# Selective-scan layer of a four-layer network: scan in double steps with its first states in a column of the tile, mean and residual moved to TensorE

## The chip, the cores and the metric

The kernel runs on one core of a Trainium2 chip. The time is device microseconds of one execution; the time of a version is the median of its runs. A profile is of one execution, whose own time is given beside its span. The engines are named PE (TensorE), DVE (VectorE), ACT (ScalarE), POOL (GpSimd) and SP (SyncE, which here only issues DMAs).

## The reference

A network of four residual layers on x of shape (3, 256, 48, 48), fp32: `x = x + layer(groupnorm(x))`. Layer 0 is a block with attention, layer 1 a convolution with mixed kernels, layer 2 a plain convolution. Layer 3, which the change touches, is a selective scan (Mamba) over the 2304 pixels of each image, taken as a sequence; cut to what matters:

```
xn    = layernorm over the 256 channels
x_in  = in_proj(xn)[:512];  z = in_proj(xn)[512:]
u     = silu(causal convolution of x_in, 4 taps)
dt_raw, B, C = x_proj(u)                 # 16, 16 and 16 rows
dt    = softplus(dt_proj(dt_raw) + bias)
# for each of 512 channels d and 16 states n, over time t:
h[d,n] = h[d,n] * exp(dt[d] * A[d,n]) + dt[d] * B[n] * u[d]
y[d]   = sum over n of h[d,n] * C[n]
out   = out_proj((y + u * D) * silu(z))
```

## The kernel before, in words

Layers 0 to 2 come first (lines 344 to 990) and are not touched. Layer 3 begins at line 995. Each image is cut into 6 chunks of 384 pixels (`CH`), 18 chunks in all, in the order of `todo`. The 512 channels are four blocks `m`; the 16 states are four groups `g` of four. A scan works on 128 partitions: 32 channels by 4 states of the group, so that block m and group g need four scans, `q` = 0 to 3. A **step** is (chunk, m, g): 16 steps a chunk, 288 steps.

For one step:

- `fill` (line 1285) makes the scan's second input dt * u * B in a tile `hs` of four rows of 384. DVE writes q 0 and 1 from PSUM (`ps_r`, which `spread_pe`, line 1268, makes with PE by replicating channels); POOL writes q 2 and 3 from SBUF (`dtur`, which `spread`, line 1258, brings by DMA from a copy in DRAM, together with `dtr` for the decays).
- `decay` (line 1296): ACT writes exp(dt * A) of one q into a PSUM tile; three such tiles take turns, so ACT is up to three scans ahead.
- Line 1360: DVE's scan of one q, in place in `hs`. Its start is 0.0 in the first chunk of an image, else a column of `hst`, which ACT copied from the same step's last column in the chunk before (line 1372).
- Line 1375: POOL multiplies the whole `hs` with C into `hc`.
- `add_states` (line 1309): PE sums over states, four matmuls of 32 output rows into `ps_y`, after a first one that adds u * D. It is called two steps later. `gate` (line 1325) multiplies with silu(z) on DVE.

In the program's order a step is: fill of the next step, spread_pe (at g = 2), four scans with the decay three scans ahead behind each, the copy to hst, the product with C, add_states of the step two before.

Between them lie the stages that prepare the next two chunks and finish the one before. Lists written out by hand (lines 1207 to 1251) give each stage the step number j of the chunk (0 to 15), a place in the step (MID: after the second scan; LATE: after the product with C; PE_: at the step's end) and the chunk it works for. Among them, for the chunk two ahead, layer norm: `group_scale` (ACT, j 12), `channel_mean` (PE, j 12), `centre` (DVE subtracts the mean from `xg`, ACT squares, j 13), `channel_mean` of the squares (PE, j 13), `inverse_root` (ACT), `normalise` (DVE), `tokens` (ACT). For the next chunk: `taps` (convolution and input projection as eight matmuls of PE for each block) and `take_u` (ACT), `silu` (ACT: a table load, the Silu, a table load back), `project_u`, `take_dbc` (ACT and DMAs of B and C), `project_dt`, `softplus` (three ACT passes), `take_dt` (DVE, then an ACT copy, then DMAs), `project_z`, `take_z`. For the chunk before: `residual` (DMA of x into `ot`), `project_y` (PE), `store` (DVE adds `ot`, DMA out). All these matmuls use one pair of PSUM banks, `bank` (`ps_g`).

`keep_order` (line 1397) fixes on PE, DVE, ACT and POOL exactly the order in which the program writes the instructions. So what counts on each engine is what stands ahead in its queue. The helper `run` (line 1253) calls the stages of a place in the order of the lists.

Of the kernel before, what the change touches and what calls it, by code (L numbers as in the profile page):

```python
# [9 lines left out]
F32 = mybir.dt.float32  # L10
I32 = mybir.dt.int32
AF = mybir.ActivationFunctionType
ALU = mybir.AluOpType
AX = mybir.AxisListType
PSUM = bass.MemoryType.PSUM

P = 128
# [3 lines left out]
CT = 2  # L21
# [4 lines left out]
CH = 384  # L26
NCH = N // CH
# [7 lines left out]
DI = 4  # L35
# [47 lines left out]
def net(  # L83
# [20 lines left out]
    nc = tc.nc  # L104
# [13 lines left out]
    def v(name, i=0, n=1):  # L118
# [3 lines left out]
    ident = const.tile([P, P], F32, name="ident")  # L122
# [6 lines left out]
        out=gview, in_=gview, pattern=[[-8, 16], [0, 8]], compare_op=ALU.is_ge,  # L129
# [3 lines left out]
        out=gview, in_=gview, pattern=[[8, 16], [0, 8]], compare_op=ALU.is_ge,  # L133
# [4 lines left out]
    mean2 = const.tile([P, P], F32, name="mean2")  # L138
# [205 lines left out]
    with ExitStack() as l0:  # L344
# [39 lines left out]
        with ExitStack() as p1:  # L384
# [3 lines left out]
            for b in ORDER:  # L388
# [12 lines left out]
                for m in range(2):  # L401
                    for ct in range(CT):
                        nc.tensor.matmul(
                            pb[:, m : m + 1], w("cv1", ct * 256 + m * P, P), sh[:, ct : ct + 1],
                            start=ct == 0, stop=ct == CT - 1,
                        )
                bb = small.tile([P, 2], F32, name="bb")
# [3 lines left out]
                for c in range(NCH):  # L411
                    for m, dst in ((0, y1), (1, cur[b])):
                        pm = ps.tile([P, 512], F32, tag="s", name="ps_y")
                        for ct in range(CT):
                            nc.tensor.matmul(
                                pm[:, :CH], ws[:, ct, m * P : (m + 1) * P], chunk(xb[:, ct, :], c),
                                start=ct == 0, stop=ct == CT - 1,
# [67 lines left out]
        with ExitStack() as p2:  # L485
# [9 lines left out]
            for i in range(NB):  # L495
# [268 lines left out]
                for mt in range(0, NT, 2):  # L764
                    pv = pair()
                    for j in range(2):
                        nc.tensor.matmul(
                            pv[:, j, :384], cur[2][:, (mt + j) * P : (mt + j + 1) * P], wn[2],
                            start=True, stop=True,
# [19 lines left out]
                if i + 1 < NB:  # L789
# [4 lines left out]
                    for b in ORDER:  # L794
                        for c in range(NCH):
                            f = hidden(b, c)
# [67 lines left out]
        i = NB - 1  # L864
        mark = listed[-1]
        chunks = [(b, c) for b in ORDER for c in range(NCH)]
# [15 lines left out]
        for n, b in enumerate(ORDER):  # L882
            held = None
            for c in range(NCH):
                f = hidden(b, c)
# [31 lines left out]
    with ExitStack() as l1:  # L917
# [55 lines left out]
        for n, (k, h) in enumerate(halves):  # L973
            layer, b = units[k]
# [17 lines left out]

    with ExitStack() as l3:
        wp = l3.enter_context(tc.tile_pool(name="w3", bufs=1))
        act = l3.enter_context(tc.tile_pool(name="act", bufs=2))
        scn = l3.enter_context(tc.tile_pool(name="scn", bufs=2))
        psd = l3.enter_context(tc.tile_pool(name="psd", bufs=3, space=PSUM))
        psr = l3.enter_context(tc.tile_pool(name="psr", bufs=1, space=PSUM))  # L1000
        psg = l3.enter_context(tc.tile_pool(name="psg", bufs=1, space=PSUM))
        psy = l3.enter_context(tc.tile_pool(name="psy", bufs=1, space=PSUM))
# [32 lines left out]
            )  # L1035
        fold = rep[:, 0, :]

        diag = wp.tile([P, DI, P], F32, name="diag")
        for m in range(DI):
            nc.vector.tensor_scalar(diag[:, m, :], ident, v("D", m), None, ALU.mult)  # L1040
# [3 lines left out]
        def fetch(at):  # L1044
            k = chunks[at] = Chunk()
            k.b, k.c = todo[at]
            k.before = chunks.get(at - 1)
            k.xg = act.tile([P, CT, CH], F32, name="xg")
            nc.sync.dma_start(k.xg, xd[k.b][:, :, k.c * CH : (k.c + 1) * CH])
# [14 lines left out]
                    bias=sh[:, ct : ct + 1], scale=sc[:, ct : ct + 1],  # L1064
                )

        def channel_mean(src, j):
            for ct in range(CT):
                nc.tensor.matmul(  # L1069
                    bank[:, j, :CH], mean2, src[:, ct, :], start=ct == 0, stop=ct == CT - 1  # L1070
                )

        def centre(k):
            mu = bank[:, 0, :CH].unsqueeze(1).broadcast_to([P, CT, CH])
            nc.vector.tensor_tensor(k.xg, k.xg, mu, ALU.subtract)
            k.sq = act.tile([P, CT, CH], F32, name="sq", bufs=1)
            nc.scalar.activation(k.sq, k.xg, AF.Square)

# [107 lines left out]
        def project_y(k, mo):  # L1186
            for m in range(DI):
                nc.tensor.matmul(  # L1188
                    bank[:, mo, :CH], w("out", m * 256 + mo * P, P), k.sz[:, m, :],
                    start=m == 0, stop=m == DI - 1,  # L1190
                )

        def residual(k):
            k.ot = act.tile([P, CT, CH], F32, name="ot")
            nc.sync.dma_start(k.ot, xd[k.b][:, :, k.c * CH : (k.c + 1) * CH])

        def store(k, mo):
            o = k.ot[:, mo, :]
            nc.vector.tensor_tensor(o, bank[:, mo, :CH], o, ALU.add)  # L1199
            nc.sync.dma_start(  # L1200
                out[k.b, mo * P : (mo + 1) * P, k.c * CH : (k.c + 1) * CH], o
            )

        MID, LATE, PE_ = range(3)
        plan = [
            (12, MID, 2, group_scale),
            (12, PE_, 2, lambda k: channel_mean(k.xg, 0)),
            (13, MID, 2, centre),  # L1210
            (13, PE_, 2, lambda k: channel_mean(k.sq, 1)),
            (14, MID, 2, inverse_root),
            (14, LATE, 2, normalise),
            (15, MID, 2, tokens),
# [22 lines left out]
            (4, MID, -1, residual),  # L1237
            (6, PE_, -1, lambda k: project_y(k, 0)),
            (6, PE_, -1, lambda k: project_y(k, 1)),
            (7, LATE, -1, lambda k: store(k, 0)),  # L1240
            (7, LATE, -1, lambda k: store(k, 1)),
        ]

        gating = [
# [8 lines left out]
        def run(at, j, place):  # L1253
            for when, where, rel, stage in after + plan + gating:
                if (when, where) == (j, place) and 0 <= at + rel < len(todo):
                    stage(chunks[at + rel])

        def spread(k, m):

            dtr = scn.tile([P, 4, CH], F32, name="dtr")  # L1260
            dtur = scn.tile([P, 2, CH], F32, name="dtur")
            for i in range(4):
                r = slice(32 * i, 32 * i + 32)
                nc.sync.dma_start(dtr[r], k.dtd[:, m, :].rearrange("(q d) n -> d q n", d=32))
                nc.sync.dma_start(dtur[r], k.dtud[:, m, :].rearrange("(q d) n -> d q n", d=32))
            return dtr, dtur
# [10 lines left out]
            k.ps = t  # L1277


        steps = [(at, m, g) for at in range(len(todo)) for m in range(DI) for g in range(4)]  # L1280
        chunks = {}
        tiles = {}
        state = {}

        def fill(s):

            at, m, g = steps[s]
            k = chunks[at]
            bb = k.bc[0][:, g, :].unsqueeze(1).broadcast_to([P, 2, CH])
            hs = tiles[s] = scn.tile([P, 4, CH], F32, name="hs", bufs=4)  # L1290
            nc.vector.tensor_tensor(hs[:, 0:2, :], k.ps[:, :, :CH], bb, ALU.mult)  # L1291
            nc.gpsimd.tensor_tensor(hs[:, 2:4, :], k.rows[m][1], bb, ALU.mult)  # L1292

        decays = []

        def decay(n):

            s, q = divmod(n, 4)
            if s >= len(steps):
                return  # L1300
            at, m, g = steps[s]
            da = psd.tile([P, 512], F32, tag="d", name="ps_da")
            col = (m * 4 + g) * 4 + q
            nc.scalar.activation(  # L1304
                da[:, :CH], chunks[at].rows[m][0][:, q, :], AF.Exp, scale=amat[:, col : col + 1]
            )
            decays.append(da)

        def add_states(s):

            at, m, g = steps[s]
            k = chunks[at]
            hc = tiles.pop(s)
            if g == 0:
                k.y_ps = psy.tile([P, 512], F32, name="ps_y")
                nc.tensor.matmul(
                    k.y_ps[:, :CH], diag[:, m, :], k.u[:, m, :], start=True, stop=False
                )
            for q in range(4):
                nc.tensor.matmul(  # L1320
                    k.y_ps[32 * q : 32 * q + 32, :CH], fold, hc[:, q, :],
                    start=False, stop=g == 3,
                )

        def gate(at, m):
            k = chunks[at]
            nc.vector.tensor_tensor(k.sz[:, m, :], k.y_ps[:, :CH], k.sz[:, m, :], ALU.mult)
# [17 lines left out]
        for _, _, _, stage in gating:  # L1345
            stage(k)

        for s, (at, m, g) in enumerate(steps):
            k = chunks[at]
            j = 4 * m + g  # L1350
            if j == 2 and at + 2 <= last:
                fetch(at + 2)
            if s + 1 < len(steps):
                fill(s + 1)

            if g == 2 and s + 2 < len(steps):
                spread_pe(chunks[steps[s + 2][0]], steps[s + 2][1])
            hs = tiles[s]
            for q in range(4):
                nc.vector.tensor_tensor_scan(  # L1360
                    hs[:, q, :], decays[q][:, :CH], hs[:, q, :],
                    0.0 if k.c == 0 else state[m, g][:, q : q + 1], ALU.mult, ALU.add,
                )
                decay(4 * s + q + 3)
                if q == 1:
                    if g == 2 and s >= 6:
                        gate(*steps[s - 6][:2])
                    run(at, j, MID)
            del decays[:4]
            if k.c < NCH - 1:  # L1370
                h = state[m, g] = wp.tile([P, 4], F32, name=f"hst{m}{g}")
                nc.scalar.copy(h.unsqueeze(2), hs[:, :, CH - 1 : CH])
            cb = k.bc[1][:, g, :].unsqueeze(1).broadcast_to([P, 4, CH])
            hc = tiles[s] = scn.tile([P, 4, CH], F32, name="hc", bufs=3)
            nc.gpsimd.tensor_tensor(hc, hs, cb, ALU.mult)  # L1375
            run(at, j, LATE)
            if s >= 2:
                add_states(s - 2)
            run(at, j, PE_)
            if g == 1 and m + 1 < DI:  # L1380
                k.rows[m + 1] = spread(k, m + 1)
            elif g == 1 and at < last:
                chunks[at + 1].rows = {0: spread(chunks[at + 1], 0)}
        end = len(steps) - 1
        add_states(end - 1)
        add_states(end)
        gate(*steps[end][:2])
        k = chunks[last]
        residual(k)
        for mo in range(2):  # L1390
            project_y(k, mo)
        for mo in range(2):
            store(k, mo)
        keep_order(tc, listed, mark)


# [110 lines left out]
```

## Time and profile before

| | |
|---|---|
| median of 3 runs | 3835.44 us (3830.97 to 3836.76) |
| the profiled execution | 3840.89 us, span 3839.1 us |
| busy in the span | PE 84%, DVE 84%, ACT 58%, POOL 40% |
| mean granted clock of PE | 0.901 |
| first fill of POOL in layer 3 | at 2245.35 us |
| first scan, end of the last scan | 2257.74 us, 3819.57 us |
| DMA | 266.50 MB, mean 69 GB/s |

The page gives the busy time of each engine, then forty slices of the span with the busy share in tenths, DMA queues, the chain that ended last, and the costliest groups of instructions. A group's line has the source line, the engine, the operation, out<-in with shapes, how often, then the busy time in us and the mean ns of one, and after the second bar the idle time of the engine just before these instructions and what ended it. A timeline line has start and length in us, the engine, the line and the operation, and how many were merged. Times in a timeline are from the start of the span.

### The profile page before, as it was taken

The numbers are of one execution on the slowest core, as the hardware profiler recorded it, in microseconds if no ns is written. First come the engines' busy times: TensorE is split into PE (matmuls) and PEld (weight loads), VectorE is DVE, ScalarE is ACT, GpSimd is POOL, SyncE is SP. The second block draws the span as 40 slices with busy tenths as digits, with TensorE's granted clock in tenths as the row PEclk, the third lists the DMA queues.
The fourth block names the chain that finished last, engine by engine and source line by source line (L and its number), as shares of the span: only waits on it lengthen the run. The fifth ranks groups of instructions, "written<-read, shape, count | busy, mean of one in ns | idle before, by whom it ended". The sixth has DMA issues, their size and how long they took to land. (4 is left out here: it accounts for less than half of the span.)

```text
span 3839.1 us, 45642 instructions
## 1 busy us (share of the span) xinstructions
PE 3232.1 (84%) x17010; PEld 1406.6 (37%) x17010; DVE 3221.5 (84%) x3518; ACT 2228.0 (58%) x3216; POOL 1554.8 (40%) x674
## 2 busy tenths in 40 slices
PE   7999999999999988677699757777878878777874
PEld 4323232432323234355577523333333333333331
DVE  4898989779899963799988349999999999999997
ACT  2788787668878762210000147666677666667763
POOL 0000000000000002100000039999999999999998
PEclk9999999999999999888899878888888888888886
DMA  4000000000000015555101133434443433343441
GB/s 170 3 1 1 1 2 1 26 13 1 1 1 2 1 57 173 174 177 177 45 25 42 59 71 100 105 99 104 103 104 91 108 91 99 100 112 92 111 100 34
DMA packets 149962, 266.50 MB, mean 69 GB/s; under 512 B 23441, under 2 KB 123601, under 8 KB 147170
## 3 DMA queue, kind: packets, MB, share of 16 engines
q1 hardware_dynamic: 137634, 245.80, 22.9%
q10 hardware_dynamic: 12096, 17.70, 1.4%
q8 instruction: 135, 2.21, 0.2%
q14 instruction: 97, 0.79, 0.1%
HBM read 216.31 MB, written 46.89 MB: 69 GB/s over the span
## 5 line engine op out<-in xcount | busy, mean ns | idle before, releaser
L587 ACT ACTIVATE pt<-ps_s 128x1024 f32<-128x1024 f32 x972 | 939.0, 1022 | 237.3 <-PE ps_s L583 219.9
L1375 POOL TENSOR_TENSOR hc<-hs,bc 128x1536 f32<-128x1536 f32 x288 | 991.4, 3443 | 85.6 <-DVE hs L1360 56.7
L663 DVE TENSOR_TENSOR part<-part,pt 128x2048 f32<-128x2048 f32 x396 | 906.6, 2289 | 78.4 <-ACT pt L587 53.8
L1360 DVE TENSOR_TENSOR_SCAN hs<-ps_da,hst,hs 128x384 f32<-128x384 f32 x960 | 909.8, 997 | 23.5 <-ACT ps_da L1304 19.9
L1304 ACT ACTIVATE ps_da<-dtr,amat 128x384 f32<-128x384 f32 x1152 | 657.1, 581 | 359.0 <-DVE hs L1360 339.9
L160 POOL TENSOR_TENSOR rstd<-ve,mhalf 128x2 f32<-128x2 f32 (+1 forms) x26 | 17.5, 675 | 1661.7 <-DVE ve L158 1661.7
L583 PE MATMUL ps_s<-q,kt 32*128 32x512 f32 (+1 forms) x4320 | 616.4, 595 | 2.3 <-DVE q L544 0.9
L1292 POOL TENSOR_TENSOR hs<-dtur,bc 128x768 f32<-128x768 f32 x288 | 523.8, 1819 | 77.5 <-DMA dtr<-dtd 77.5
L596 PE MATMUL acc<-pt,vt 128*32 128x512 f32 (+1 forms) x4320 | 523.5, 563 | 8.2 <-DVE o L643 8.0
L927 PE MATMUL ps_c<-vt,u 128*128 128x288 f32 x1728 | 437.8, 417 | 92.9 <-DVE u L257 55.1
L1105 PE MATMUL ps_g<-xn,wtap 128*128 128x384 f32 x1152 | 392.2, 493 | 36.3 <-ACT u L1112 31.3
L927 PEld LDWEIGHTS ps_c<-vt,u 128*128 128x128 f32 x1728 | 335.4, 195 | 190.0 <-issue 56.3
L583 PEld LDWEIGHTS ps_s<-q,kt 32*128 32x128 f32 x4320 | 220.2, 184 | 389.6 <-issue 230.0
L1320 PE MATMUL ps_y<-hc,rep 128*32 128x384 f32 x2304 | 293.5, 596 | 34.6 <-POOL hc L1375 32.7
L1291 DVE TENSOR_TENSOR hs<-ps_r,bc 128x768 f32<-128x768 f32 x288 | 269.1, 934 | 61.8 <-PE ps_r L1273 61.8
L1105 PEld LDWEIGHTS ps_g<-xn,wtap 128*128 128x128 f32 x1152 | 212.7, 189 | 220.1 <-ACT u L1112 54.9
L596 PEld LDWEIGHTS acc<-pt,vt 128*32 128x32 f32 x4320 | 95.7, 108 | 364.3 <-issue 328.5
L943 ACT COPY cb<-ps_c 128x288 f32<-128x288 f32 x48 | 19.0, 395 | 355.5 <-PE ps_c L927 258.5
L1360 DVE TENSOR_TENSOR_SCAN hs<-ps_da,hs 128x384 f32<-128x384 f32 x192 | 170.7, 937 | 17.9 <-ACT ps_da L1304 17.7
L1176 PE MATMUL ps_g<-xn,w3sb 128*128 128x384 f32 x288 | 133.8, 608 | 58.1 <-ACT sz L1184 43.3
L1069 PE MATMUL ps_g<-xg,mean 128*128 128x384 f32 x72 | 52.7, 887 | 105.3 <-ACT dt L1167 78.2
L1320 PEld LDWEIGHTS ps_y<-hc,rep 128*32 128x32 f32 x2304 | 51.3, 118 | 239.1 <-POOL hc L1375 113.5
(204 smaller groups left out, 3265.5 us busy)
## 6 DMA issues: line engine op xcount, KB each, us to landing
wconv<-in_we SPq DMA_DIRECT2D x144, 384.0 KB, 4.3
dtr<-dtd SPq DMA_DIRECT2D x288, 192.0 KB, 3.6
bc<-bcd SPq DMA_DIRECT2D x144, 192.0 KB, 5.9
dtur<-dtud SPq DMA_DIRECT2D x288, 96.0 KB, 2.7
dtd<-dt SPq DMA_DIRECT2D x18, 768.0 KB, 3.5
yc<-ycat ACTq DMA_DIRECT2D x18, 576.0 KB, 5.3
xb<-in_x SPq DMA_DIRECT2D x6, 1152.0 KB, 11.1
ycat<-cur SPq DMA_DIRECT2D x6, 1152.0 KB, 4.9
```

The lines of the kernel that those rows point to most:

```text
L583: nc.tensor.matmul(s[:, j, cols], kt[r, mt * P : (mt + 1) * P], q[r, :n], start=True, stop=True,)
L587: nc.scalar.activation(p[:, h0 : h0 + 2, :], s, AF.Exp)
L596: nc.tensor.matmul(acc[h * HD : (h + 1) * HD, :n], vt[:, mt, g * P + h * HD : g * P + (h + 1) * HD], p[:, h, cols], start=mt == 0, stop=mt ...
L663: nc.vector.tensor_tensor(part, first_p if group == 1 else part, p, ALU.add)
L927: nc.tensor.matmul(pc[:, :HN], u[:, i, dy, ct, m * P : (m + 1) * P], vt[:, i, ct, dy * TW : dy * TW + HN], start=ct == 0 and dy == 0, stop ...
L1105: nc.tensor.matmul(bank[:, m % 2, :CH], wtap[:, tap, ct, m * P : (m + 1) * P], k.xn[:, ct, tap : tap + CH], start=tap == 0 and ct == 0, st ...
L1291: nc.vector.tensor_tensor(hs[:, 0:2, :], k.ps[:, :, :CH], bb, ALU.mult)
L1292: nc.gpsimd.tensor_tensor(hs[:, 2:4, :], k.rows[m][1], bb, ALU.mult)
L1304: nc.scalar.activation(da[:, :CH], chunks[at].rows[m][0][:, q, :], AF.Exp, scale=amat[:, col : col + 1])
L1320: nc.tensor.matmul(k.y_ps[32 * q : 32 * q + 32, :CH], fold, hc[:, q, :], start=False, stop=g == 3,)
L1360: nc.vector.tensor_tensor_scan(hs[:, q, :], decays[q][:, :CH], hs[:, q, :], 0.0 if k.c == 0 else state[m, g][:, q : q + 1], ALU.mult, ALU.add,
L1375: nc.gpsimd.tensor_tensor(hc, hs, cb, ALU.mult)
```

## The change

A step becomes a **double step** (chunk, m, h), h = 0 or 1, of two groups g and eight scans: 8 a chunk, 144 in all. The scans run in the order (g0 q0, q1), (g1 q0, q1), (g0 q2, q3), (g1 q2, q3).

- `hs` has rows of 385: column 0 takes the first state (`first_states`, an ACT copy of eight columns, of zeros in an image's first chunk), columns 1 to 384 the input. The scan runs over 385 columns with the constant start 0.0; the decay tiles have a zero in column 0, set once, and `decay` writes columns 1 to 384. `last_states` copies column 384 for the next chunk.
- The three decay tiles are three named ones instead of a pool's rotation.
- `fill` is one DVE and one POOL instruction for two groups, the product with C one POOL instruction. There are two `hs` and two `hc` tiles of double size, where there were four and three.
- The order in a double step: eight scans with the decay three ahead behind each; then the next step's fill, `first_states` of the next step, `last_states`, the product with C, add_states of the step before, and spread_pe (at h = 0). MID comes after parts 1 and 5, LATE after parts 3 and 7, PE_ after part 3 and at the end; spread (the DMAs) after part 3 at h = 0.
- Layer norm: `less_mean` gives x minus its mean directly in `bank`, with four matmuls whose weights are identity minus 1/256 and minus 1/256; `centre` is then an ACT copy and the Square.
- `project_y` adds the residual with a matmul by the identity; `store` is one ACT copy of both halves.

```diff
-        psd = l3.enter_context(tc.tile_pool(name="psd", bufs=3, space=PSUM))
+        psd = l3.enter_context(tc.tile_pool(name="psd", bufs=1, space=PSUM))
...
+        less = wp.tile([P, 2, P], F32, name="less")
+        nc.vector.tensor_tensor(less[:, 0, :], ident, mean2, ALU.subtract)
+        nc.vector.tensor_scalar(less[:, 1, :], mean2, -1.0, None, ALU.mult)
+        zero = wp.tile([P, 8], F32, name="zero")
+        nc.vector.memset(zero, 0.0)
...
+        def less_mean(k):
+            for to in range(CT):
+                for ct in range(CT):
+                    nc.tensor.matmul(
+                        bank[:, to, :CH], less[:, int(to != ct), :], k.xg[:, ct, :],
+                        start=ct == 0, stop=ct == CT - 1,
+                    )
...
         def centre(k):
-            mu = bank[:, 0, :CH].unsqueeze(1).broadcast_to([P, CT, CH])
-            nc.vector.tensor_tensor(k.xg, k.xg, mu, ALU.subtract)
+            nc.scalar.copy(k.xg, bank[:, :, :CH])
...
+            nc.tensor.matmul(bank[:, mo, :CH], ident, k.ot[:, mo, :], start=False, stop=True)
...
+        def store(k):
+            nc.scalar.copy(k.ot, bank[:, :, :CH])
+            for mo in range(CT):
+                nc.sync.dma_start(
+                    out[k.b, mo * P : (mo + 1) * P, k.c * CH : (k.c + 1) * CH], k.ot[:, mo, :]
+                )
...
-            hs = tiles[s] = scn.tile([P, 4, CH], F32, name="hs", bufs=4)
-            nc.vector.tensor_tensor(hs[:, 0:2, :], k.ps[:, :, :CH], bb, ALU.mult)
-            nc.gpsimd.tensor_tensor(hs[:, 2:4, :], k.rows[m][1], bb, ALU.mult)
+            hs = tiles[s] = scn.tile([P, 2, 4, CH + 1], F32, name="hs")
+            bb = k.bc[0][:, 2 * h : 2 * h + 2, :].unsqueeze(2).broadcast_to([P, 2, 2, CH])
+            nc.vector.tensor_tensor(
+                hs[:, :, 0:2, 1:],
+                k.ps[:, :, :CH].unsqueeze(1).broadcast_to([P, 2, 2, CH]), bb, ALU.mult,
+            )
+            nc.gpsimd.tensor_tensor(
+                hs[:, :, 2:4, 1:],
+                k.rows[m][1].unsqueeze(1).broadcast_to([P, 2, 2, CH]), bb, ALU.mult,
+            )
...
+        def first_states(s):
+            at, m, h = steps[s]
+            src = zero if chunks[at].c == 0 else state[m, h]
+            nc.scalar.copy(tiles[s][:, :, :, 0], src.rearrange("p (g q) -> p g q", g=2))
...
+        def scan(s, part):
+            g, q = parts_of_step[part]
+            b = tiles[s][:, g, q, :]
+            nc.vector.tensor_tensor_scan(
+                b, slots[(8 * s + part) % 3][:, : CH + 1], b, 0.0, ALU.mult, ALU.add
+            )
...
+        for s, (at, m, h) in enumerate(steps):
+            if m == 0 and h == 1 and at + 2 <= last:
+                fetch(at + 2)
+            for part in range(8):
+                j = 4 * m + 2 * h + part // 4
+                scan(s, part)
+                decay(8 * s + part + 3)
+                if part % 4 == 1:
+                    if h == 1 and part == 1 and s >= 3:
+                        gate(*steps[s - 3][:2])
+                    run(at, j, MID)
+                if part % 4 == 3:
+                    run(at, j, LATE)
+                if part == 3:
+                    run(at, j, PE_)
...
             if s + 1 < len(steps):
                 fill(s + 1)
+                first_states(s + 1)
+            last_states(s)
+            times_c(s)
+            if s >= 1:
+                add_states(s - 1)
+            run(at, 4 * m + 2 * h + 1, PE_)
+
+            if h == 0 and s + 2 < len(steps):
+                spread_pe(chunks[steps[s + 2][0]], steps[s + 2][1])
```

## The prediction

> **What bounds the kernel now.** I began with the page's forty slices: GpSimd (POOL) is idle until the scan layer and at 9 from then on, so the change lives in the last 41% of the span. Then I read busy time by stretch, in the scan layer's steady part. After the stretch and its length come busy time and number of instructions of each engine, the granted clock, the DMA share and GB/s.
>
> ```profile
> 2500.00:3000.00 500.00, 399.69 (x1568) 167.40 (x1569) 461.88 (x530) 345.13 (x618) 478.95 (x187) 0.86 0.39 99
> 3000.00:3500.00 500.00, 395.75 (x1558) 162.61 (x1556) 460.40 (x530) 347.15 (x619) 476.37 (x185) 0.85 0.41 102
> ```
>
> POOL is busy 95.5%, DVE 92%, ACT 69%, PE 79%: two engines close to full, handing tiles to each other. The groups by form of the stretch 2500 to 3700 (222 POOL steps, so 5.405 us a step and 86.5 us a chunk of 16 steps) show what they do:
>
> ```profile
> L1375 POOL TENSOR_TENSOR hc<-hs,bc 128x1536 f32<-128x1536 f32 x222 | 764.5, 3444 | 53.4 <-DVE hs L1360 43.4 <-DMA bc<-bcd 8.1 <-POOL hs L1292 0.2
> L1292 POOL TENSOR_TENSOR hs<-dtur,bc 128x768 f32<-128x768 f32 x222 | 404.0, 1820 | 0.0
> L1360 DVE TENSOR_TENSOR_SCAN hs<-ps_da,hst,hs 128x384 f32<-128x384 f32 x758 | 718.5, 997 | 16.6 <-ACT ps_da L1304 15.8
> L1360 DVE TENSOR_TENSOR_SCAN hs<-ps_da,hs 128x384 f32<-128x384 f32 x128 | 113.7, 937 | 6.2 <-ACT ps_da L1304 6.1
> L1291 DVE TENSOR_TENSOR hs<-ps_r,bc 128x768 f32<-128x768 f32 x221 | 206.5, 934 | 49.3 <-PE ps_r L1273 49.3
> ```
>
> POOL waits 53.4 us (3.8 a chunk), nearly all for scans; DVE waits once a chunk 3.5 us for ps_r (49.3/14). A scan that reads its start from hst costs 997 ns, one with a constant 937. Since instructions overlap a little, sums go by distances between starts, from the timelines of DVE and POOL:
>
> ```profile
> 3006.51 0.93 DVE L1291 TENSOR_TENSOR hs<-ps_r,bc 128x768 f32<-128x768 f32 x1
> 3007.36 3.73 DVE L1360 TENSOR_TENSOR_SCAN hs<-ps_da,hst,hs 128x384 f32<-128x384 f32 x4
> 3011.01 0.93 DVE L1291 TENSOR_TENSOR hs<-ps_r,bc 128x768 f32<-128x768 f32 x1
> ...
> 2786.11 3.49 DVE L1360 TENSOR_TENSOR_SCAN hs<-ps_da,hs 128x384 f32<-128x384 f32 x4
> 2789.51 0.93 DVE L1291 TENSOR_TENSOR hs<-ps_r,bc 128x768 f32<-128x768 f32 x1
> ```
> ```profile
> 3010.15 1.83 POOL L1292 TENSOR_TENSOR hs<-dtur,bc 128x768 f32<-128x768 f32 x1
> 3011.93 3.44 POOL L1375 TENSOR_TENSOR hc<-hs,bc 128x1536 f32<-128x1536 f32 x1
> 3015.32 1.82 POOL L1292 TENSOR_TENSOR hs<-dtur,bc 128x768 f32<-128x768 f32 x1
> ```
>
> A DVE fill takes 0.85, four scans 3.65 with hst and 3.40 without; POOL 1.78 and 3.39, 5.17 a step. On ACT a Silu is this, 4.09 us in which no decay is made:
>
> ```profile
> 2999.05 1.28 ACT L1117 ACT_TABLE_LOAD   x1
> 3000.34 1.49 ACT L1117 ACTIVATE u<-u 128x1536 f32<-128x1536 f32 x1
> 3001.84 1.28 ACT L223 ACT_TABLE_LOAD   x1
> 3003.14 1.09 ACT L1304 ACTIVATE ps_da<-dtr,amat 128x384 f32<-128x384 f32 x2
> ```
>
> **The change, part by part (us per chunk, 8 double steps).**
>
> *POOL.* Same elements in half the instructions. The two forms give (3444-1820)/768 = 2.115 ns an element, so a double fill is 1.78 + 768 x 2.115 ns = 3.40, a double product 3.39 + 1536 x 2.115 ns = 6.64: 10.04, 80.3 a chunk instead of 82.7. No row shows POOL on rows of 385. If merging saves nothing it stays 82.7; if every element costs what it does in the small form (1820/768 = 2.37 ns) it is 4608 x 2.37 = 10.9, 87.4 a chunk. I take 80.3, the slope of the same operations.
>
> *DVE.* Eight scans without hst, 0.855 each with the 385th column: 6.84. Double fill: 768x1 costs 934 and the gate's 384 (L1327) 536, so 1.036 ns an element: 0.85 + 0.80 = 1.65. Eight steps 67.9; four gates 1.8, two take_dt 3.7, normalise 0.9 (each by starts): 74.3. Centre (927) and the two adds of store (553 each) leave DVE. Before, the same sum is 16 x 4.50 + 6.4 + 1.8 = 80.2, and with 6.3 of waits makes the 86.5. So DVE's own work falls by 5.9.
>
> A fill is now followed by a scan of its own tile. Where DVE waits for its own result (L1163 then L1164) starts lie 0.99 apart, against 0.87 for a pair without a wait: 0.13 at each boundary without another wait. The Trainium skill, page "VectorE: DVE Perf Modes", section "The DRAIN you can't avoid", says the pipe empties behind every operation and that semaphores between them cost nothing extra; by it this term would be nothing. Starts 0.85 apart of operations that last 0.93 disagree with it; with the rule the chunk below would be 0.4 shorter.
>
> *ACT.* Per chunk: 8 first_states and 8 last_states for 16 hst copies (181 ns each, 0.09 when queued): no change in sum. Added: centre and store as 128x768 copies from PSUM, 0.80 each by L1167. The skill's page "ScalarE: Activation LUTs", section "Rules for kernel authors", gives adds and the like to VectorE, which it calls up to three times faster in bf16; by it centre and store would have stayed, at 1.8 a chunk more on DVE. The rows, fp32 from PSUM, have ACT at 0.80 and DVE at 0.93. Busy time is not what matters on ACT (69%) but order: first_states(s+1) is queued behind everything of part 7, and scan 0 of the next step waits for it.
>
> *PE.* less_mean is four matmuls for two, project_y ten for eight. Taps, eight matmuls, take 5.4 by the timeline (3.17 us of ACT waiting behind them), 0.68 each: +2.7 a chunk; about 63 of 84 busy. spread_pe loses its old wait: it now has a step (about 10 us) between its issue and the fill that needs it, so the 3.5 for ps_r goes.
>
> *SP.* The same DMAs; spread moves from after a step's PE work to part 3 of the first half. Its rows are needed 10 us later and land in 3.6 (dtr) and 2.7 (dtur): nothing. Less, zero and the slot memsets are made in the prologue, where DVE idles 16.9 us for L1069: nothing. Column 0 of the decay tiles is set once; the three PSUM banks and their distance of three scans stay.
>
> **What is late next.** I walk one chunk through the queues by these durations. After part 5 DVE has two scans and a fill, 3.36, until it needs first states. ACT has 0.59 for the decay it starts with, the stage, two decays 1.04, the copy 0.15.
> - Boundary 0 to 1: take_u(0) waits for taps(0), which started when take_z freed the bank (5.05 after the step's start) and end at 10.45; copies until 11.1; DVE is there at 10.5: 0.65.
> - Step 1: Silu of sz after part 1. DVE has a gate and three scans (3.0), ACT 0.59 + 4.09 + 0.53: 2.2.
> - Step 3: gate m=0 waits for add_states(1), behind taps(3) on PE: 0.75.
> - Boundary 3 to 4: 0.59 + 4.09 (Silu of u) + 1.04 + store 0.75 + 0.15 = 6.6 against 3.36: 3.3. project_y has ended by then.
> - 4 to 5 and 5 to 6: softplus 2.45 (793, 844, 843 ns) gives 4.2 against 3.36: 0.9 each, 0.3 more at the first, where project_dt waits for take_dbc.
> - 6 to 7: 0.15; 7 to 8 (tokens, take_z): 0.3; 1 to 2 and 2 to 3: none.
>
> That is 9.45 of waits; with 0.4 for own fills (three boundaries) and 0.4 for handovers (0.05 x 8) 10.25. **Chunk: 74.3 + 10.25 = 84.6**, in which POOL (80.3) waits about 4.3. Now: 86.5.
>
> The scan part of the profile runs from 2257.7 to 3819.6, 1561.8 = 18 x 86.5 + 4.8 of start. After: 18 x 84.6 + 4.8 = 1527.6, 34 less. The end grows: after the last scan the product takes 6.7 where the chain now takes 4.8 (+1.9), four more matmuls onto ps_y +1.5 (the timeline's last groups), two identity matmuls at 6.6/8 each +1.65, store -0.2, and up to 3.4 if POOL is a fill behind: +6. Sum -28 on the profiled execution's 3840.9 (span 3839.1); that execution lies 5.5 above the median, and -28 from the median 3835.4 gives **3807**.
>
> By the same formula a chunk of P us moves the time by 18 P + 10.8 - 1561.8: even at P = 86.2.
>
> **Rivals.**
> 1. *POOL alone bounds.* DVE can be about 4 us ahead (two hs tiles: its fill needs the product two steps back; then 1.65 + 6.84 + 0.8 of extras against 3.40 + 6.64 + 3.40). If ACT's lateness falls within that lead, P goes to 80.3 to 83: -106 to -57, 3729 to 3778. For it: POOL is already 95.5% busy. Against: my waits come in a row, steps 3 to 5.
> 2. *Nothing comes through.* A chunk that starts from zero has the cheap scans already (64 x 0.06 = 3.8 less DVE work), and yet the DVE timeline has its first scan at 2786.11 and the next chunk's at 2871.55: 85.4, only 1.1 less. The rest returns as waits for PE and decays. P 85.8 to 86.6: within 8.
> 3. *First states are the new bound: slower.* Each of 8 boundaries puts ACT's queue between fill and scan 0. I have 0.81 on average; beyond 1.1 (11.9 of waits in all) the change loses. A PE clock of 0.81, as in 2400 to 2500, lengthens every matmul that ACT waits for by 6%; with that, or one more stage late per chunk, 1.1 to 1.5 gives P 86.7 to 89: +10 to +51, 3845 to 3886. POOL at 87.4 for padded rows ends at the same place (+22), with POOL never waiting.
> That it isn't doing what it says is small: scans over 385 columns with a zero decay in column 0 start from that column.
>
> **How the numbers follow.** Forecast (P 83 to 85.8) 0.46; POOL alone 0.16; nothing 0.12; slower 0.26. A measurement of this kernel tells 0.2%, 7.7 us, from no change: faster 0.62, same 0.12, slower 0.26. The forecast's own range is 3778 to 3828. For 8 in 10 I reach to P = 82 (3760, half of the first rival) and to P = 87.8 (3865, most of the third); below and above lie about 0.08 and 0.1.
>
> **What would show it.** Right: scans at about 940 ns with no hst, products near 6.69 and fills 3.44 on POOL, the ps_r wait gone, DVE waiting 6 to 7 us a chunk for ACT's first states, most after Silu of u, POOL idle about 4. Wrong: POOL forms above 6.9 and 3.6 (rows of 385 cost), ACT waits at every boundary (third rival), POOL idle under 1 (first), or a DVE fill above 1.75.

## The result, and the profile after

The changed kernel takes **3871.63 us**, median of four runs (3869.70 to 3874.02), against 3836.10 (3830.97 to 3837.24) for four runs of the kernel before beside it: ratio 1.0096, 95% interval 1.0078 to 1.0113. It is 35.5 us slower, outside the range on record; the third rival happened.

The profiled execution took 3869.70, span 3867.8, 28.7 more than the span before. Three pieces make that up: the first scan starts at 2264.24 instead of 2257.74 (+6.5), the scans take 1579.7 instead of 1561.8 (+17.8), and what follows the last scan 23.9 instead of 19.5 (+4.4). The steady chunk shown below takes 87.84 us (its first scans at 3019.55 and 3107.39), where a chunk of before took 86.5. It is one of the shorter ones: counted from take_dt to take_dt, sixteen chunks in a row take 88.7 us on average (87.7 to 91.4), against 86.8 in the kernel before.

Busy time by stretch in the kernel after, columns as for the kernel before (PE, PEld, DVE, ACT, POOL, clock, DMA, GB/s):

```profile
2500.00:3000.00 500.00, 400.90 (x1574) 182.06 (x1575) 422.85 (x457) 348.52 (x624) 428.50 (x91) 0.86 0.39 98
3000.00:3500.00 500.00, 391.28 (x1565) 177.34 (x1564) 423.53 (x458) 349.94 (x623) 433.04 (x92) 0.86 0.40 100
```

POOL fell from 95.5% to 86%, DVE from 92% to 85%, PE and ACT stand within 1% of where they were, and the kernel is slower: the two full engines were given less to do and now stand idle. The groups by form, 2500 to 3700, say for whom:

```profile
L1347 DVE TENSOR_TENSOR_SCAN hs<-ps_da,hs 128x385 f32<-128x385 f32 x867 | 758.5, 937 | 181.4 <-ACT hs L1323 142.6 <-ACT ps_da L1339 36.0
L1355 POOL TENSOR_TENSOR hc<-hs,bc 128x3072 f32<-128x3072 f32 x108 | 665.8, 6165 | 134.6 <-DVE hs L1347 134.6
...
L1315 POOL TENSOR_TENSOR hs<-dtur,bc 128x1536 f32<-128x1536 f32 x109 | 374.4, 3435 | 30.7 <-DMA dtur<-dtud 19.7 <-ACT ps_da L1339 3.6
...
L1311 DVE TENSOR_TENSOR hs<-ps_r,bc 128x1536 f32<-128x1536 f32 x108 | 187.0, 1732 | 0.0
...
L1323 ACT COPY hs<-hst 128x8 f32<-128x8 f32 x92 | 17.7, 192 | 0.0
```

The idle time in front of the scans went from 22.8 us (16.6 + 6.2) to 181.4, and 142.6 of that ends with L1323, `first_states`: a copy of 0.19 us that itself waits for no other engine (0.0). It is late because of what stands ahead of it in ACT's queue, as the lines further down show. POOL then waits 134.6 us for scans. The ps_r wait in front of the fill, 49.3 before, is gone.

The chunk on DVE's timeline (start, length, engine, line, operation; in brackets the idle time ahead and what ended it):

```profile
3019.55 6.91 DVE L1347 TENSOR_TENSOR_SCAN hs<-ps_da,hs 128x385 f32<-128x385 f32 x8 [3.31 <-ACT hs L1323]
3026.38 1.73 DVE L1311 TENSOR_TENSOR hs<-ps_r,bc 128x1536 f32<-128x1536 f32 x1
3029.52 1.81 DVE L1347 TENSOR_TENSOR_SCAN hs<-ps_da,hs 128x385 f32<-128x385 f32 x2 [1.41 <-ACT hs L1323]
...
3041.30 1.81 DVE L1347 TENSOR_TENSOR_SCAN hs<-ps_da,hs 128x385 f32<-128x385 f32 x2 [0.89 <-ACT hs L1323]
...
3053.61 1.81 DVE L1347 TENSOR_TENSOR_SCAN hs<-ps_da,hs 128x385 f32<-128x385 f32 x2 [1.90 <-ACT hs L1323]
...
3061.91 1.73 DVE L1311 TENSOR_TENSOR hs<-ps_r,bc 128x1536 f32<-128x1536 f32 x1
3063.75 6.91 DVE L1347 TENSOR_TENSOR_SCAN hs<-ps_da,hs 128x385 f32<-128x385 f32 x8
...
3073.20 1.81 DVE L1347 TENSOR_TENSOR_SCAN hs<-ps_da,hs 128x385 f32<-128x385 f32 x2 [0.89 <-ACT hs L1323]
...
3080.41 2.66 DVE L1347 TENSOR_TENSOR_SCAN hs<-ps_da,hs 128x385 f32<-128x385 f32 x3 [2.40 <-ACT ps_da L1339]
3082.99 1.73 DVE L1311 TENSOR_TENSOR hs<-ps_r,bc 128x1536 f32<-128x1536 f32 x1
3084.82 6.91 DVE L1347 TENSOR_TENSOR_SCAN hs<-ps_da,hs 128x385 f32<-128x385 f32 x8
...
3094.88 1.81 DVE L1347 TENSOR_TENSOR_SCAN hs<-ps_da,hs 128x385 f32<-128x385 f32 x2 [1.50 <-ACT hs L1323]
...
3107.39 0.96 DVE L1347 TENSOR_TENSOR_SCAN hs<-ps_da,hs 128x385 f32<-128x385 f32 x1 [3.48 <-ACT hs L1323]
```

From 3019.55 on the brackets add up to 1.41 + 0.89 + 1.90 + 0.89 + 2.40 + 1.50 + 3.48 = 12.47 us; the other 75.4 are work. Over the sixteen chunks the brackets are 13.3 us a chunk. ACT's timeline shows the last of them, ahead of 3107.39:

```profile
3101.18 1.28 ACT L1132 ACT_TABLE_LOAD   x1
3102.47 1.48 ACT L1132 ACTIVATE u<-u 128x1536 f32<-128x1536 f32 x1
3103.97 1.28 ACT L223 ACT_TABLE_LOAD   x1
3105.27 1.09 ACT L1339 ACTIVATE ps_da<-dtr,amat 128x384 f32<-128x384 f32 x2
3106.45 0.80 ACT L1214 COPY ot<-ps_g 128x768 f32<-128x768 f32 x1
3107.14 0.21 ACT L1323 COPY hs<-hst 128x8 f32<-128x8 f32 x1
```

DVE's fill ended at 3103.90. The copy needs nothing that was not there by then, but stands behind a Silu with its two table loads, two decays and the new store.

### The profile page after: what moved, and what is told of

Read it like the earlier page. It is cut to its first block, busy times and chain, and to the rows that moved or that the text cites. A ratio compares the mean times of both kernels' runs of the same rounds, so it can differ in the third digit from the quotient of the medians.

```text
span 3867.8 us, 45732 instructions
## 1 busy us (share of the span) xinstructions
PE 3247.4 (84%) x17154; PEld 1463.4 (38%) x17154; DVE 3128.3 (81%) x3326; ACT 2262.0 (58%) x3276; POOL 1441.6 (37%) x386
## 5 line engine op out<-in xcount | busy, mean ns | idle before, releaser
L1347 DVE TENSOR_TENSOR_SCAN hs<-ps_da,hs 128x385 f32<-128x385 f32 x1152 | 1007.3, 937 | 240.7 <-ACT hs L1323 186.2
L1355 POOL TENSOR_TENSOR hc<-hs,bc 128x3072 f32<-128x3072 f32 x144 | 887.4, 6163 | 186.7 <-DVE hs L1347 165.9
L1315 POOL TENSOR_TENSOR hs<-dtur,bc 128x1536 f32<-128x1536 f32 x144 | 494.7, 3436 | 115.8 <-DMA dtr<-dtd 77.8
L1372 PE MATMUL ps_y<-hc,rep 128*32 128x384 f32 x2304 | 258.1, 573 | 41.5 <-POOL hc L1355 38.1
L1311 DVE TENSOR_TENSOR hs<-ps_r,bc 128x1536 f32<-128x1536 f32 x144 | 249.4, 1732 | 0.0
L1164 PE MATMUL ps_g<-dbc,dtsb 17*128 17x384 f32 x144 | 80.6, 695 | 113.0 <-ACT dt L1182 92.9
L1078 PE MATMUL ps_g<-xg,less 128*128 128x384 f32 x144 | 91.1, 809 | 94.8 <-ACT dt L1182 67.5
L1203 PE MATMUL ps_g<-sz,w3sb 128*128 128x384 f32 x288 | 126.6, 594 | 40.6 <-ACT u L1127 40.6
L1191 PE MATMUL ps_g<-xn,w3sb 128*128 128x384 f32 x288 | 119.2, 550 | 47.3 <-DVE xg L1101 40.7
```

The lines of the kernel that those rows point to most:

```text
L1311: nc.vector.tensor_tensor(hs[:, :, 0:2, 1:], k.ps[:, :, :CH].unsqueeze(1).broadcast_to([P, 2, 2, CH]), bb, ALU.mult,)
L1315: nc.gpsimd.tensor_tensor(hs[:, :, 2:4, 1:], k.rows[m][1].unsqueeze(1).broadcast_to([P, 2, 2, CH]), bb, ALU.mult,)
L1347: nc.vector.tensor_tensor_scan(b, slots[(8 * s + part) % 3][:, : CH + 1], b, 0.0, ALU.mult, ALU.add)
L1355: nc.gpsimd.tensor_tensor(hc, tiles[s][:, :, :, 1:], cb.broadcast_to([P, 2, 4, CH]), ALU.mult)
L1372: nc.tensor.matmul(k.y_ps[32 * q : 32 * q + 32, :CH], fold, hc[:, g, q, :], start=False, stop=h == 1 and g == 1,)
```

## The experiments

Theories at the start: **A**, the loss is the place of `first_states` in ACT's queue; **B**, it is the layer-norm and residual part; **C**, a double step is too coarse a unit whatever stands in the queue. D and E, inside B, came after the first four runs. In the table, ratio and difference are to the kernel before, run beside it; the difference is that of the medians. The ratio of e1 holds one run of 3908.01; its medians alone give 1.0098.

| run | what it is | median us | ratio, 95% interval | difference |
|---|---|---|---|---|
| e1_scan_only | the change without layer norm and residual | 3873.01 | 1.0121 (1.0071 to 1.0172) | +37 |
| e2_ln_only | before with layer norm and residual alone | 3868.42 | 1.0083 (1.0066 to 1.0100) | +33 |
| e3_first_on_pool | the change, `first_states` on POOL | 3755.20 | 0.9789 (0.9773 to 0.9805) | -80 |
| e4_take_u2_early | the change, take_u(2) earlier | 3871.33 | 1.0090 (1.0073 to 1.0107) | +36 |
| e5_scan_first_pool | e1 with `first_states` on POOL | 3785.02 | 0.9858 (0.9840 to 0.9876) | -54 |
| e6_mean_only | before with the mean alone | 3845.82 | 1.0018 (1.0008 to 1.0027) | +7 |
| e7_residual_only | before with residual and store alone | 3864.94 | 1.0065 (1.0045 to 1.0086) | +26 |
| e8_padded_rows | before with rows of 385 in hs | 3835.46 | 0.9991 (0.9981 to 1.0002) | none shown |
| e9_pointer_start | the change, scans start from hst | 3793.57 | 0.9883 (0.9866 to 0.9899) | -45 |
| e10_first_early_act | the change, `first_states` early on ACT | 3755.65 | 0.9783 (0.9767 to 0.9800) | -83 |
| e11_pool_mean_only | e3, residual and store on DVE again | 3772.85 | 0.9831 (0.9815 to 0.9848) | -66 |
| e12_silu_late | e10, Silu of sz later | 3757.96 | 0.9785 (0.9763 to 0.9807) | -80 |

### Which part loses: e1 and e2

The first takes back layer norm and residual, the second takes only them.

```diff
 e1: -        def less_mean(k):          +        def channel_mean(src, j):
     -            nc.scalar.copy(k.xg, bank[:, :, :CH])
     +            nc.vector.tensor_tensor(k.xg, k.xg, mu, ALU.subtract)
     -            nc.tensor.matmul(bank[:, mo, :CH], ident, k.ot[:, mo, :], start=False, stop=True)
     -            nc.scalar.copy(k.ot, bank[:, :, :CH])
     +            nc.vector.tensor_tensor(o, bank[:, mo, :CH], o, ALU.add)
 e2: the reverse, in the kernel before
```

> The double-step scan alone: centre and store are on DVE again, mean by two matmuls, no matmul by the identity. Theory A (the loss is first_states in ACT's queue between fill and scan 0): most boundary waits stay; the one behind centre (1.9 us a chunk) and the 0.8 of store before first states go, DVE gets 1.8 of work and about 0.8 of waiting for project_y back, so a chunk of about 88 as now: 3860 to 3880. Theory B (the loss is the layer-norm and residual part, by its matmuls and its ACT copies): at most 3836.

> Before with the mean, centre and residual by TensorE and ACT, single steps as they were. Theory A: DVE loses 1.8 us a chunk, ACT gets 1.6 where no first_states stand behind it: 3815 to 3845. Theory B: 3855 to 3875, the whole loss.

The scan part alone loses 37 us, as A had it, with 86.5 us of waits for `first_states` in the stretch 2500 to 3700. But layer norm and residual alone lose 33 us, where A had 3815 to 3845 us: B is right about that kernel. Each part loses as much as both together, so neither can be read from the whole.

### Does the place of first_states carry the loss: e3, e10, e9

```diff
 e3:  in fill, after the tile is made:
 +            first_states(s)
 ...
 -            nc.scalar.copy(tiles[s][:, :, :, 0], src.rearrange("p (g q) -> p g q", g=2))
 +            nc.gpsimd.tensor_copy(tiles[s][:, :, :, 0], src.rearrange("p (g q) -> p g q", g=2))
 ...
 -                first_states(s + 1)
```

> The change with first_states as a copy by POOL ahead of its own fill, nothing else. Theory A: scan 0 no longer waits for ACT's queue; of some 11 us of waits a chunk the Silu of sz (2.4) and about 0.8 behind the Silu of u stay, POOL gets 8 x 0.2; a chunk of 80.5 to 82, and the 6.5 us of the prologue go too: 3740 to 3770, well under both kernels. Theory C (two double tiles are too coarse a handover between DVE and POOL, whoever writes column 0): less than 30 us under the change, 3840 to 3872.

```diff
 e10: +        def open_tile(s):
      +            tiles[s] = scn.tile([P, 2, 4, CH + 1], F32, name="hs")
      +            first_states(s)
      ...
      +                if part == 5 and s + 1 < len(steps):
      +                    open_tile(s + 1)
      ...
      -                first_states(s + 1)
```

> The change with first_states still on ACT, but written after the decay of part 5, ahead of part 5's stages and of the two decays and LATE stages that stood before it. Theory A, that only the place in the queue matters: as on POOL, within 20 us of 3755. If ACT now waits there for POOL to release the tile, and the decays behind it with it: 3790 to 3860.

```diff
 e9:  -                b, slots[(8 * s + part) % 3][:, : CH + 1], b, 0.0, ALU.mult, ALU.add
      +                b, slots[(8 * s + part) % 3][:, 1 : CH + 1], b,
      +                0.0 if chunks[at].c == 0 else state[m, h][:, col : col + 1], ALU.mult, ALU.add,
      ...
      -                first_states(s + 1)
```

> The change with scans that start from a column of hst again, over 384 columns: double steps, merged POOL and DVE instructions, the layer-norm and residual part, and no first_states at all. Theory A (the loss sits in first_states' place in ACT's queue, not in the double step): 64 x 0.06 = 3.8 us a chunk more on DVE than with first_states on POOL (3755), at most 70 more, and POOL's 1.5 less: 3760 to 3825, under both kernels. Theory C (the double step is too coarse): 3860 or more.

All three came as A had it; C falls. e3 moves the copy to another engine, e10 leaves it on ACT and writes it two parts earlier: 3755.20 and 3755.65. So it is neither the copy's cost nor its engine, but what stands ahead of it. The same boundary as at 3107.39, now in e3, on DVE's timeline:

```profile
3035.98 1.73 DVE L1312 TENSOR_TENSOR hs<-ps_r,bc 128x1536 f32<-128x1536 f32 x1
3037.85 0.96 DVE L1348 TENSOR_TENSOR_SCAN hs<-ps_da,hs 128x385 f32<-128x385 f32 x1
3039.71 6.17 DVE L1348 TENSOR_TENSOR_SCAN hs<-ps_da,hs 128x385 f32<-128x385 f32 x7 [0.90 <-ACT ps_da L1340]
```

ACT does the same Silu and store, but scan 0 now needs only its decay, which was made three scans ahead: 0.90 us are lost instead of 3.48. The three decay tiles were a cushion that `first_states` had bypassed. The groups of e3, 2500 to 3700:

```profile
L1348 DVE TENSOR_TENSOR_SCAN hs<-ps_da,hs 128x385 f32<-128x385 f32 x941 | 830.3, 940 | 77.3 <-ACT ps_da L1340 61.4 <-DVE hs L1312 0.5
...
L1356 POOL TENSOR_TENSOR hc<-hs,bc 128x3072 f32<-128x3072 f32 x118 | 727.0, 6161 | 26.5 <-DVE hs L1348 18.3 <-PE ps_y L1373 7.8
```

The chunk is 81.9 us (first scans at 3008.05 and 3089.96). e9, run beside e10, has no `first_states` at all and is 38 us slower than it, because its scans cost more again:

```profile
L1344 DVE TENSOR_TENSOR_SCAN hs<-ps_da,hst,hs 128x384 f32<-128x384 f32 x790 | 740.9, 998 | 53.9 <-ACT ps_da L1334 43.2 <-ACT hst L1324 0.5
```

998 against 940 ns, 960 times in an execution, is 56 us of DVE work; 38 reach the end. So the column is worth its copy once the copy is early.

### A wait taken away singly: e4 and e12

```diff
 e4:  -            (5, MID, 1, lambda k: take_u(k, 2)),
      +            (4, LATE, 1, lambda k: take_u(k, 2)),
 e12: -            (2, MID, 0, lambda k: silu(k.sz)),
      +            (3, LATE, 0, lambda k: silu(k.sz)),
```

> The change with take_u(2) moved from after part 5 to after part 3 of the same double step, so that it stands ahead of taps(3) in the program. Theory A with its detail that take_u(2) waits for taps(3) because the two banks are one tile: the 1.5 us wait at the boundary of double steps 2 and 3 goes, 18 x 1.5 = 27 us: 3840 to 3850. If that wait is for taps(2) itself, or is given back at the next boundary: 3865 to 3872.

The forecast of 27 us missed: nothing was gained. The wait did go, but taps(3) now waits 1.53 us for take_u(2), which reads the same `bank`, as PE's timeline in e4 shows:

```profile
3091.24 5.43 PE L1120 MATMUL ps_g<-xn,wtap 128*128 128x384 f32 x16 [1.53 <-ACT u L1127]
3096.60 1.50 PE L1372 MATMUL ps_y<-hc,rep 128*32 128x384 f32 x16
```

The add_states behind it (L1372) ends that much later, and the gate, which did not wait before, waits for it on DVE:

```profile
3095.22 1.81 DVE L1347 TENSOR_TENSOR_SCAN hs<-ps_da,hs 128x385 f32<-128x385 f32 x2
3098.16 0.56 DVE L1379 TENSOR_TENSOR sz<-ps_y,sz 128x384 f32<-128x384 f32 x1 [1.13 <-PE ps_y L1372]
```

Over 2500 to 3700 waits for `first_states` fell by 17 us (142.6 to 125.7) and 14.4 appeared at the gate. This is the other branch of the expectation, the wait given back at the next place.

> The version with first_states early on ACT (3756), and the Silu of sz moved from after part 1 to after part 7 of the same double step, where DVE has a fill and three scans (4.4) ahead of it instead of three scans (2.6) against the 4.6 us in which ACT makes no decay. If lateness of ACT at given places is what is left: the 2.3 us wait a chunk goes to about 0.3, 18 x 2 = 36 us, 3715 to 3735. If POOL bounds by now, or the wait comes back elsewhere: 3745 to 3760.

The 36 us missed too: 3757.96 against 3755.65, ratios 0.9785 (0.9763 to 0.9807) and 0.9783 (0.9767 to 0.9800). In e10 the Silu costs one wait of 2.33 us, on DVE's timeline:

```profile
3019.47 2.66 DVE L1351 TENSOR_TENSOR_SCAN hs<-ps_da,hs 128x385 f32<-128x385 f32 x3 [2.33 <-ACT ps_da L1343]
```

In e12 it still costs one, of 0.93 instead of the 0.3 expected: ACT makes the decays that DVE lacks there only behind the Silu's second table load.

```profile
3027.91 1.28 ACT L223 ACT_TABLE_LOAD   x1
...
3029.31 2.19 ACT L1343 ACTIVATE ps_da<-dtr,amat 128x384 f32<-128x384 f32 x4
```

DVE's timeline of e12 has that wait, and a longer one after it:

```profile
3029.92 4.36 DVE L1351 TENSOR_TENSOR_SCAN hs<-ps_da,hs 128x385 f32<-128x385 f32 x5 [0.93 <-ACT ps_da L1343]
...
3038.27 0.96 DVE L1351 TENSOR_TENSOR_SCAN hs<-ps_da,hs 128x385 f32<-128x385 f32 x1 [1.27 <-ACT ps_da L1343]
```

The second, 1.27, was 0.34 in e10; there ACT stands behind taps for take_u (3.85 us in e12, 2.92 in e10), with the decays behind that. Waits for decays fell only from 65.3 to 57.9 us, and DVE now waits 4.7 for ps_r. The chunk stays as it was: from take_dt to take_dt most take 81.93 us in e10, 81.92 in e12 and 81.91 in e3. What holds all three at that length is open; that one chain of ACT and PE stages is late at several places, whichever shows, fits them but is not shown.

### Layer norm and residual: e6, e7, e5, e11

D said that their loss comes from store and what follows it on PE, E that it comes from centre behind less_mean. The edits are the two halves of e2's.

> Before with only the mean and centre by TensorE and ACT. Theory D (the loss of the layer-norm and residual part comes from store: ten matmuls, then an ACT copy, and only then project_u, so that B and C arrive late): 3830 to 3845. Theory E (it comes from centre, an ACT copy that waits for four slow matmuls with the decays behind it): 3855 to 3870.

> Before with only the residual by TensorE and store on ACT. Theory D: 3855 to 3870, with POOL waiting for the DMA of bc as in the run of both. Theory E: 3825 to 3840.

D is right about most of it: 7 and 26 us, together the 33 of e2 (e6 lies 0.8 us above the range that D gave it). In e7, project_u, whose banks store must free, on PE's timeline:

```profile
3010.01 0.81 PE L1192 MATMUL ps_g<-ot,ident 128*128 128x384 f32 x2
...
3013.62 4.52 PE L1123 MATMUL ps_g<-u,w3sb 128*96 128x384 f32 x8 [2.02 <-ACT ot L1199]
...
3056.74 2.85 PE L1176 MATMUL ps_g<-xn,w3sb 128*128 128x384 f32 x8 [2.66 <-ACT sz L1184]
```

and the same eight matmuls in the kernel before, where DVE made the store:

```profile
3002.21 2.79 PE L1123 MATMUL ps_g<-u,w3sb 128*96 128x384 f32 x8 [0.42 <-DVE ot L1199]
```

ACT's copy is 0.79 us long, but PE waits 2.02, and then takes 4.52 for what took 2.79. Windows of PE alone in e7 (length, busy, clock, DMA, GB/s), ahead of the wait and after it:

```profile
3004.00:3011.00 7.00, 7.00 (x28) 1.00 0.56 140
3013.60:3018.20 4.60, 4.58 (x12) 0.63 0.39 128
```

The granted clock fell from 1.00 to 0.63; behind the longer gap ahead of 3056.74 it did not fall (last section). So B and C reach their tiles late, and POOL, busy 95.5% of that stretch, waits for them 40.7 us (8.1 before):

```profile
L1375 POOL TENSOR_TENSOR hc<-hs,bc 128x1536 f32<-128x1536 f32 x218 | 750.6, 3443 | 73.5 <-DMA bc<-bcd 40.7 <-DVE hs L1360 31.3
```

That the loss runs through POOL is not shown. DVE's waits for decays rose as well, from 21.9 to 65.3 us, since ACT waits 27.0 us for project_u with the decays behind it, and e8 below finds POOL not to be the bound in the kernel before.

> The double-step scan with first_states on POOL, and centre, residual and store as they were before the change. It asks what the layer-norm and residual part is worth once the boundary waits are gone (3755 with it). If its lateness on ACT costs here what it costs in single steps (33 us): 3715 to 3735. If taking 1.8 us a chunk off DVE pays: 3770 to 3790.

> first_states on POOL, mean and centre by TensorE and ACT, but residual and store on DVE as before the change. With both parts it took 3755, with neither 3785. If the residual part costs here as in single steps (25 to 30 us, through project_u behind store): 3720 to 3740, the fastest. If what it takes off DVE (0.9 us a chunk and the wait for project_y) counts for more: 3760 to 3785.

With `first_states` out of the way the same edits gain: e3 is 26 us below e5 by the medians' differences to the kernel before (-80 and -54). Of these the residual is worth 14 by the same differences (e11 -66), or 17 against e10, run beside e11 (3772.85 and 3755.65), though e10 has `first_states` on ACT. So e11's case of a residual that costs is refuted. A likely reason is DVE's time: in e11 it waits 15.1 us over 14 chunks for project_y (1.1 a chunk) and makes the two adds of 0.55 itself. POOL waits only 0.3 us for bc in e3. The rule cited ahead, adds to VectorE ("ScalarE: Activation LUTs", "Rules for kernel authors", the Trainium skill), fits the kernel before, where leaving it cost 26 us, and not e11, where keeping it cost 14 to 17. Both edits also move the addition itself to PE, so they are no test of the two engines' speed; they fit that what decides here is which queue has room.

### Was POOL the bound before: e8

```diff
-            hs = tiles[s] = scn.tile([P, 4, CH], F32, name="hs", bufs=4)
+            hs = tiles[s] = scn.tile([P, 4, CH + 1], F32, name="hs", bufs=4)[:, :, 1:]
```

> Before with rows of 385 in hs, the first column unused, and nothing else. The change's product took 6.16 us where the slope gave 6.69. If rows of 385 make it cheaper: the product takes 3.05 to 3.15 instead of 3.44, POOL is busy 5 us a chunk less, and the time falls by what DVE's waits leave of that, 3800 to 3830. If it is the merging: 3.44, 3830 to 3840.

Nothing but the row distance changes, and the product gets 8% cheaper:

```profile
L1375 POOL TENSOR_TENSOR hc<-hs,bc 128x1536 f32<-128x1536 f32 x223 | 708.2, 3176 | 109.8 <-DVE hs L1360 90.9 <-DMA bc<-bcd 17.0 <-PE ps_y L1320 1.1
```

288 x (3.444 - 3.176) = 77 us of POOL's work are gone, POOL idles 109.8 instead of 53.4 in the stretch, and the time does not move (0.9981 to 1.0002); the 3800 to 3830 expected did not come. An engine 95.5% busy was not the bound.

## Why the prediction was wrong

It named the mechanism and its break-even, and gave it 0.26. What failed is the step **"What is late next"**: it had 9.45 us of waits a chunk, and 12.47 were measured in the chunk above (13.3 on average). The break-even of 11.9 holds the 0.8 of own fills and handovers too, so for the waits alone it is 11.1. By the same terms the third rival's 1.1 to 1.5 us a boundary give P of about 86.9 to 90, not 86.7 to 89; measured in this chunk were 1.26 (10.07 over 8 boundaries). The work held: 75.4 against 74.3 + 0.8. That the forecast's formula gives +30 with P = 87.84, where the span has +28.7, is partly luck: with the mean of 88.7 it gives +45. What it lacks is the stretch from the last chunk's take_dt on, where no next chunk is prepared: the kernel after takes 103.3 us from there to the end of the last scan, the one before 110.1.

| wait | forecast | measured |
|---|---|---|
| 0 to 1 | 0.65 | 0.89 |
| step 1, Silu of sz | 2.2 | 2.40 |
| 2 to 3 | 0 | **1.50** |
| gate m = 0 | 0.75 | 0 |
| 3 to 4 | 3.3 | 3.48 |
| 4 to 5, 5 to 6 | 1.2, 0.9 | 1.41, 0.89 |
| 6 to 7 | 0.15 | **1.90** |
| 7 to 8 | 0.3 | 0 |

Two terms, 1.50 and 1.75 too small, make more than the 3.0 that were missing in this chunk.

**2 to 3.** I had taken taps(2) to be long done when take_u(2) is due. ACT's timeline after shows otherwise:

```profile
3093.17 0.58 ACT L1127 ACTIVATE u<-ps_g,vec 128x384 f32<-128x384 f32 x1 [2.52 <-PE ps_g L1120]
```

and PE's what it waited for:

```profile
3082.54 10.59 PE L1120 MATMUL ps_g<-xn,wtap 128*128 128x384 f32 x32 [0.19 <-ACT u L1127]
```

32 records are taps(2) and taps(3) together, and the copy runs when the last has ended, 5.3 us (half of 10.59) after the ones it needs. taps(3) stands ahead of it in the program and writes the other half of the same `bank`. That the wait comes from there is shown by e4, where take_u(2) is written ahead of taps(3) and no longer waits. I could have read it from the trace of before, in whose waits ACT stands 60.4 us behind these matmuls, 24 times.

**6 to 7.** centre waits for less_mean, for which I put down 0.68 a matmul: 2.7 for its four. PE's timeline after:

```profile
3045.84 4.92 PE L1078 MATMUL ps_g<-xg,less 128*128 128x384 f32 x8 [4.09 <-ACT dt L1182]
```

and ACT's, where centre waits for the end of it:

```profile
3050.79 0.80 ACT L1090 COPY xg<-ps_g 128x768 f32<-128x768 f32 x1 [1.81 <-PE ps_g L1078]
```

The time of these matmuls was sized with taps, which run in a row (5.43 for eight, at a granted clock of 1.00 from 3067 to 3072). less_mean runs at 0.57 from 3045.8 to 3050.7 and takes 4.92, 1.23 a matmul. At 0.68 it would have ended at 3048.56, before ACT was free at 3048.98, and of the 1.90 only 0.1 would be left, near the 0.15 forecast. The page of before already had the mean's matmuls at 887 ns a record and the taps' at 493 (two records are one matmul).

**Start and end.** I put the start at nothing. It cost 6.5, and here too it is the queue: `first_states(0)` is written behind the stages of the prologue. DVE's first scans in the kernel after:

```profile
2264.24 4.36 DVE L1347 TENSOR_TENSOR_SCAN hs<-ps_da,hs 128x385 f32<-128x385 f32 x5 [6.68 <-ACT hs L1323]
```

The end grew by 4.4, forecast 6.

**What held.** Scans without hst at 937 ns; POOL's fill at 3.44; the ps_r wait gone; the waits behind both Silus and softplus within 0.2. The own fill cost a little more than forecast: in the chunk above scan 0 starts 0.10 after its fill has ended (3082.99 + 1.73, 3084.82), where independent scans overlap by 0.08 (937 ns long, 853 apart). The Trainium skill's rule that a semaphore between two operations costs nothing ("VectorE: DVE Perf Modes", "The DRAIN you can't avoid") does not agree with that: 0.18 a boundary, forecast 0.13. POOL's product was cheaper, 6.16 instead of 6.69, but the fewer busy us only became idle ones.

**The rivals.** The third happened, by the way it described. The time of the first, 3729 to 3778 with a chunk of 80.3 to 83, is where e3 and e10 stand (81.9 in e3), but that POOL alone bounds there is not shown: the 80.3 rest on a product of 6.64 by starts, and in e3 POOL's own work is 9.80 us a double step (two products at 3027.79 and 3037.59 without a wait between), 78.4 a chunk, with DVE waiting 5.2 us a chunk for ACT. So the number is in its range partly by luck. The gain forecast was there; one copy's place in a queue gave it back with more.

## What to carry to other kernels

A cheap instruction that another engine waits for is priced by what stands ahead of it in its in-order queue, not by its own 0.2 us; issue it as soon as its inputs exist, or on an engine whose queue has room. Before a chain of waits is summed, look for the wait of before that shows how long each stage really takes there, after idle time and behind a neighbour's half of a shared tile. Change the place and the work in separate kernels: two edits that each lost 33 to 37 us gained 80 together once one copy was moved.

## What the runs showed of the hardware

- **PE's clock halves behind some gaps and not behind others.** In e7 PE idled 2.02 us from 3011.6 on; the granted clock was 1.00 up to 3014.0 and 0.50 from 3014.5 to 3017.5, and project_u took 4.52 us instead of 2.79. In the same trace PE idled 2.66 us ahead of 3056.74, the clock stayed at 1.00, and eight matmuls took 2.85. In the kernel after it was 0.50 already from 3038 to 3042, ahead of the 4.09 us without work, and less_mean followed at 0.57. So the length of the gap just before does not decide alone; what does is open here. The Trainium skill, "TensorE: Matmul & The Clock Gate", Part 1, has a cold clock of one half after an idle window of about 3.4 us: the half agrees, and 2.02 us were enough once.
- **Rows of 385 make POOL's product cheaper**: 3176 ns instead of 3444 in e8 with nothing else changed, and twice the elements in one instruction 6161 to 6165. The fill into such rows took 3435, what the forecast had from rows of 384. Why is open.
- **The start of a scan costs by its kind**: 998 ns from a column (e9), 937 to 940 with a constant and one more column, in the same order of work; in e9 itself the scans of an image's first chunk, over 384 columns from a constant, take 937.
